# Two graph layers in one kernel: constants and tests at other places, other turns of the tiles for gathered rows, lists spread over three pairs

## The chip, the cores and the metric

The kernel runs on one core of one Trainium2 chip. The metric is the device time of the whole program in microseconds (us), as the median of several runs.

## What is computed

```
def layer0(x, adj):                       # x: 2708 x 1024, adj: 2708 x 2708 of 0 and 1
    q, k, v = x @ Wq.T + bq, x @ Wk.T + bk, x @ Wv.T + bv
    z = (q @ k.T) / sqrt(1024) * adj
    z = where(z == 0, -10000, z)
    return relu(softmax(z, axis=1) @ v)
x = layernorm(x + layer0(x, adj))
x = layernorm(x + (adj @ (x @ w1) + b1))
```

The adjacency is sparse and its degrees fall steeply with the row number: a few rows have many neighbours, most have a few, some have one or none.

## The kernel before

**The work.** Scores are needed only between a row and its neighbours. With M made once from Wq and Wk, a row's scores are the products of its row of y = xM (a broadcast row is added to it) with the rows of x of its neighbours. So the kernel first lists the neighbours of every row, and then gathers rows by indirect DMAs, which POOL (GpSimd) issues. The 22 blocks of 128 rows stand in two families, the first 8 and the other 14; inside a family rows are sorted by degree, and `SLOTS` says how many neighbours a block has room for. Rows of more neighbours go to a block of its own, the hub.

**The order of time.** (1) to 127 us: weights are loaded and M is made on PE, while DVE lists columns of the adjacency matrix. (2) 127 to 247 us: y of the first family, in four pairs (`y_pair(b)` for b = 0, 2, 4, 6). A pair is `pair_products` (L324), seven half products of a Strassen kind with sums that POOL makes beforehand (`y_sums_of`); PE's matmuls are at L300, and the sums that DVE adds to them at L322. DVE lists the last columns in the gaps: `list_columns` on DVE (L237), `count_columns` on ACT (L253). `sort_begin(f)` sorts a family by degree, `sort_end(f)` needs a small matmul on PE (L671) and gives the records, and `records_out` (L700) writes one record for each block by an indirect DMA, and then loads the table `tabs` (L710). A gather needs its block's table. (3) 247 to 460 us, the y stage: y of the other 14 blocks, block by block (L380; the last one at L431), copied from PSUM by ACT (L320) and stored by SP (L371). Beside it runs the attention of the first family's blocks and of the hub: ACT copies a broadcast row into a tile `yg` (L475), a gather adds the row of y to it (L464), the neighbours' rows of x are gathered into tiles `g` (L480), DVE makes a score from each (`score`, L1004), ACT the exponentials (L1040, L1131), and DVE the weighted sum `r` from the same tiles (L1061, L1138). (4) 461 to 747 us: the sums are turned by PE and multiplied by Wv, again in pairs; x is added (L1202), and ACT and DVE make the layernorm, whose rows POOL scatters to `x1_d` (L910). (5) 747 to 770 us: the last scatter, the first gathers from `x1_d`. (6) to 1070 us, layer 1: neighbours' rows of x1 are gathered and summed by DVE (L1429, L1432), turned by PE (L923), multiplied by w1, normed and scattered.

**What sets the order.** Attention of the blocks is cut into jobs that a planner runs between PE's blocks as their credit allows. Each engine runs its instructions in the order that results. `follow(put, what)` makes an instruction wait for an earlier one; `products` is the list of the last matmuls of PE's products, so that `products[-1]` is the newest and `products[-2]` the one before. `between[n]` holds what is to be issued behind product number n.

**Tiles.** A pool with `bufs=n` gives n tiles in turn, and a new use of one waits until its last reader is done. Gathered rows of x have `G1` = 9 tiles `g`; while there are blocks of y left, `g_tile` takes the two tiles `xr` of the pool `wp` as well, for 2 of 11. Gathered y has two tiles `yg`. Sums `r` have a ring of `RB` = 5.

**Row constants and tests.** The last part of the scores, a constant for each row, is made late: `row_constants` gathers x once more for 23 groups of rows (L464) and multiplies by a broadcast row `u_bc` on DVE (L1260), nine groups in the third-last pair of stage (4), nine in the second-last and five in the last; `single_scores` scores the two blocks with one neighbour. `test_scores` (L1271 on) then tests whether the short lists were enough and whether a score is exactly zero, for the result's flag; its work is a matmul on PE (L1287) and some 34 small steps on DVE (L1288 to L1309).

The lines that decide where these stand:

```
xg = gather_at(x, at, n, g_tile(), behind=products[-1])          # row_constants
if i == len(steps) - 3:
    u_bc = wp.tile([P, D], F32, name="u_bc", tag="yg")
    bcast_rows(u_bc, u_col)
if i >= len(steps) - 3:
    row_constants((9, 9, 5)[i - len(steps) + 3])
```

Of the kernel before, what the change touches and what calls it, by code (L numbers as in the profile page):

```python
# [9 lines left out]
F32 = mybir.dt.float32  # L10
BF16 = mybir.dt.bfloat16
I32 = mybir.dt.int32
# [9 lines left out]
P = 128  # L22
# [18 lines left out]
G1 = 9  # L41
# [40 lines left out]
def sparse_part(ctx, tc, x, xT, adj, wqT, wkT, wvT, bq, bk, bv, w1, b1, out):  # L82
# [28 lines left out]
    with es:  # L111
# [83 lines left out]
        recs = [lists.tile([P, nb, REC], I32, name=f"rec{f}") for f, nb in enumerate((FAMILY, NB - FAMILY))]  # L195
# [306 lines left out]
        def deal_hub():  # L502
# [51 lines left out]
            nc.gpsimd.dma_start(out=keys_d.rearrange("(p k) e -> p (k e)", k=KW), in_=keys)  # L554
# [14 lines left out]
            yield  # L569
            mm = p_mm.tile([P, HALF], F32, name="mm")  # L570
# [96 lines left out]
        def sort_end(f, behind=None):  # L667
            b0, nb = families[f]
            bs, NKB = slice(b0, b0 + nb), NK * nb
            before = spare_bank() if f else p_mm.tile([P, HALF], F32, name="mm")  # L670
            put = nc.tensor.matmul(before[:, :NKB], lower, hot_f[f], start=True, stop=True)  # L671
            if behind is not None:
                follow(put, behind, same=True)
            total = spare_bank()
            nc.tensor.matmul(total[:, :NKB], ones, hot_f[f], start=True, stop=True)
            one_row = lists.tile([P, NKB], F32, name=f"one_row{f}")
            nc.vector.memset(one_row, 1.0)
            upto = lists.tile([P, NKB], F32, name=f"upto{f}")
# [6 lines left out]
            pos_i = lists.tile([P, nb], I32, name=f"pos_i{f}")  # L685
            nc.vector.tensor_copy(pos_i, pos)

            rec = recs[f]
# [117 lines left out]
        y_sums = []  # L806
        t3 = yb.tile([P, DC // 2, HALF], F32, name="y_t3")
        y_sums.append(yb.tile([P, 4, DC // 2, P], F32, name="y_s0"))
        t4 = yb.tile([P, DC // 2, HALF], F32, name="y_t4")
        y_sums.append(yb.tile([P, 4, DC // 2, P], F32, name="y_s1"))  # L810
        nc.gpsimd.memset(yb.tile([P, 800], F32, name="cleared"), 0.0)
# [32 lines left out]
        sorted_late = []  # L844
# [39 lines left out]
        left_y, taken = NB - FAMILY, [0]  # L884
# [182 lines left out]
        def r_tile(b):  # L1067

            if b in FIRST:
                return wp.tile([P, D], F32, name="r", tag="t")  # L1070
            ring.append(b)
            return wp.tile([P, D], F32, name="r", bufs=RB)
# [32 lines left out]
        def attend_shares(b, got):  # L1105
# [7 lines left out]
            yg = gather_onto(b, y_bc, y_ds[0][:, :], rec[:, OFF:OFF + 1], P, wp.tile([P, D], F32, name="yg"))  # L1113
# [140 lines left out]

        def row_constants(count):
            for k in [c_left.pop(0) for _ in range(count)]:
                n = P if k in (0, NB) else rows[k]
                at = rec_h[:, ROW:ROW + 1] if k == NB else tab0[:, ROW:ROW + 1] if k == 0 else tabs[:n, k, ROW:ROW + 1]
                xg = gather_at(x, at, n, g_tile(), behind=products[-1])
                nc.vector.scalar_tensor_tensor(junkv[:n], xg[:n], 1.0, u_bc[:n], op0=ALU.mult, op1=ALU.mult,  # L1260
                                               accum_out=c_rows[:n, k:k + 1])
# [9 lines left out]
        def test_scores():  # L1271
# [5 lines left out]
            if rows[-1] < P:  # L1277
# [3 lines left out]
            nc.vector.tensor_tensor(over, degs, cap, op=ALU.is_gt)  # L1281
            s0, b0 = slot0[single[0]], single[0]
            nc.vector.scalar_tensor_tensor(nms[:, b0:b0 + len(single)], scores[:, s0:s0 + len(single)], -1.0,
                                           valid[:, b0:b0 + len(single), 0], op0=ALU.mult, op1=ALU.mult)
# [44 lines left out]
        for i, (kind, b) in enumerate(steps):  # L1329
# [29 lines left out]
            if kind == "y":  # L1359
                if FAMILY + 1 <= b < FAMILY + 7:  # L1360
                    next(deal)
                if b == FAMILY + 11:
# [18 lines left out]
            else:  # L1381
# [35 lines left out]
        def sum_rows(b, k=0, behind=None):  # L1417
            if b == "hub":
                n, tab, ok, r = P, tab_h, valid_h, part
            else:  # L1420
                n, tab, ok = (P, tab0, valid0) if b == 0 else (rows[b], tabs[:, b, :SLOTS[b]], valid[:, b, :SLOTS[b]])
                r = (cp if k else wp).tile([P, D], F32, name="r", bufs=3 if k else RB)
# [408 lines left out]
```

## Time and profile before

| | us |
|---|---|
| median of 5 runs | 1075.43 |
| lowest and highest | 1072.45, 1077.47 |
| the profiled execution | 1072.17 |
| its span | 1070.3 |
| PE busy | 962.7 (90%) |
| DVE busy | 836.2 (78%) |
| POOL busy | 557.0 (52%) |
| ACT busy | 410.8 (38%) |

The mean clock granted to PE is 0.958 of full speed. PE, DVE, ACT, POOL and SP are the five engines; POOL's busy time is the issuing of indirect DMAs. The page cuts the span into 40 slices and gives the busy share of each in tenths. A row of waits reads "engine line waited for what: us in total, times, longest". A row of a timeline reads "start, duration, engine, line, operation, tiles", and in brackets the idle time before it with what ended it. All line numbers are those of the kernel before.

### The profile page before, as it was taken

To read this page: it belongs to the slowest core of one execution; us is meant where nothing else is said; L and a number is where in the kernel's file an instruction comes from. 1 tells how busy PE (TensorE), PEld (TensorE's weight loads), DVE (VectorE), ACT (ScalarE), POOL (GpSimd) and SP (SyncE) were. 2 spreads that over 40 slices of the span, in tenths; PEclk is the share of its full clock that TensorE was granted. 3 is DMA by queue.
4 is the path that set the end of the run, shared out by engine and by line. 5 is a ranking of instruction groups with operands and counts; after the bars stand their busy time and mean duration, and the time that the engine had idled before them with its cause. 6 is when DMAs were issued, how large, how long until landed. Compare 5 with 4: busy or idle time off the path is not lost.

```text
span 1070.3 us, 10455 instructions
## 1 busy us (share of the span) xinstructions
PE 962.7 (90%) x2697; PEld 452.7 (42%) x2697; DVE 836.2 (78%) x2045; ACT 410.8 (38%) x917; POOL 557.0 (52%) x456
## 2 busy tenths in 40 slices
PE   8999869999998889899998999998299899989894
PEld 6444324444443334345544444443144344434441
DVE  8999999932857889957998899587869886868532
ACT  4453456432533324516343544422312343353521
POOL 0441452155676566105675753346588777768510
PEclk9999999999998989899999999999599999999998
DMA  9568775347987787217658874369898689987731
GB/s 353 183 205 249 221 240 165 121 148 219 278 232 247 232 252 227 103 43 234 174 157 226 226 236 159 113 237 354 289 276 238 205 294 279 327 240 218 212 110 42
DMA packets 103181, 229.21 MB, mean 214 GB/s; under 512 B 19774, under 2 KB 47174, under 8 KB 103112
## 3 DMA queue, kind: packets, MB, share of 16 engines
q0 software_dynamic: 51408, 159.09, 48.8%
q1 hardware_dynamic: 51704, 69.36, 20.1%
q8 instruction: 23, 0.38, 0.1%
q14 instruction: 46, 0.38, 0.1%
HBM read 218.08 MB, written 33.64 MB: 235 GB/s over the span
## 4 chain that ended last, share of the span: by engine, by line
PE 26%; DVE 23%; issue 20%; DMA 16%; POOL 12%; ACT 1%; POOLq 0%; SPq 0%; DVEq 0%; ACTq 0%
PE po L300 21%; POOL g L480 6%; DVE at_a L237 5%; DMA g<-in_x_dram,tabs 4%; DMA g<-x_d,tabs 3%; DVE junkv L1004 2%; PE po L380 2%; POOL xr L464 2%; DVE r L1061 2%; DMA out_dram<-t,tabs 1%; DMA a<-in_adj_dram 1%; POOL yg L464 1%; PE po L431 1%; DVE r L1432 1%; PE tr L923 1%
## 5 line engine op out<-in xcount | busy, mean ns | idle before, releaser
L380 PE MATMUL po<-m,xt 128*128 128x512 f32 x416 | 185.6, 606 | 15.1 <-ACT yo L320 15.1
L1004 DVE SCALAR_TENSOR_TENSOR junkv<-yg,g 128x1024 uint8<-128x1024 f32 x96 | 117.2, 1220 | 48.8 <-DMA g<-in_x_dram,tabs 21.4
L300 PE MATMUL po<-t,s_all 128*128 128x512 f32 x320 | 146.2, 600 | 7.6 <-DVE xr L322 6.3
L380 PEld LDWEIGHTS po<-m,xt 128*128 128x128 f32 x416 | 80.0, 195 | 118.0 <-issue 96.7
L480 POOL DMA_INDIRECT g<-in_x_dram,tabs x77 | 96.0, 1246 | 50.1 <-issue 15.2
L1432 DVE SCALAR_TENSOR_TENSOR r<-g,valid,r 128x1024 f32<-128x1024 f32 x77 | 98.2, 1280 | 21.1 <-DMA g<-x_d,tabs 18.5
L300 PEld LDWEIGHTS po<-t,s_all 128*128 128x128 f32 x320 | 60.5, 192 | 87.9 <-issue 70.2
L480 POOL DMA_INDIRECT g<-x_d,tabs x66 | 76.0, 1152 | 22.4 <-issue 14.9
L237 DVE FIND_INDEX8 at_a<-ones,a 128x8 uint16<-128x83 f32 (+3 forms) x132 | 82.6, 628 | 0.0
L966 ACT ACTIVATE junks<-t,lnm 128x1024 uint8<-128x1024 f32 (+1 forms) x40 | 45.9, 1148 | 93.8 <-DVE lnm L964 93.7
L300 PE MATMUL po<-w,rT 128*128 128x512 f32 x160 | 75.2, 611 | 3.1 <-DVE t L1469 3.1
L1061 DVE SCALAR_TENSOR_TENSOR r<-g,pr,r 128x1024 f32<-128x1024 f32 x58 | 73.7, 1279 | 4.4 <-ACT r L1059 4.3
L300 PE MATMUL po<-wv,s_all 128*128 128x512 f32 x160 | 73.9, 606 | 3.5 <-DVE t L322 3.4
L979 ACT ACTIVATE t<-t,nmr,rstd 128x1024 f32<-128x1024 f32 (+1 forms) x40 | 49.1, 1238 | 68.2 <-DVE nmr L978 68.2
L300 PE MATMUL po<-t,rT 128*128 128x512 f32 x160 | 73.3, 600 | 1.1 <-DVE t L1469 0.5
L253 ACT ACTIVATE junk<-a 128x2756 uint8<-128x2756 uint32 (+1 forms) x22 | 55.0, 2501 | 49.2 <-issue 17.0
L300 PE MATMUL po<-w,s_all 128*128 128x512 f32 x160 | 72.3, 592 | 0.0
L300 PE MATMUL po<-wv,rT 128*128 128x512 f32 x160 | 72.1, 600 | 0.0
L923 PE MATMUL tr<-ident,r 128*128 128x128 f32 x304 | 41.6, 286 | 31.6 <-DVE r L1429 23.5
L924 ACT COPY rT<-tr 128x512 f32<-128x512 f32 x76 | 41.4, 587 | 71.6 <-PE tr L923 70.3
L453 ACT ACTIVATE junka<-xt 128x128 f32<-128x128 f32 x168 | 51.7, 307 | 42.8 <-PE po L300 33.2
L464 POOL DMA_INDIRECT xr<-in_x_dram,tabs x22 | 27.5, 1252 | 63.3 <-DVE t L1202 31.2
(415 smaller groups left out, 1731.4 us busy)
## 6 DMA issues: line engine op xcount, KB each, us to landing
xt<-in_xT_dram SPq DMA_DIRECT2D x21, 512.0 KB, 5.3
y_d<-yo SPq DMA_DIRECT2D x21, 512.0 KB, 4.6
a<-in_adj_dram SPq DMA_DIRECT2D x21, 413.5 KB
a<-in_adj_dram SPq DMA_DIRECT2D x21, 338.5 KB, 3.6
a<-in_adj_dram SPq DMA_DIRECT2D x21, 263.5 KB, 4.6
wq_i<-in_wqT_dram SPq DMA_DIRECT2D x8, 512.0 KB, 4.8
wk_i<-in_wkT_dram SPq DMA_DIRECT2D x8, 512.0 KB, 10.5
wv<-in_wvT_dram SPq DMA_DIRECT2D x16, 256.0 KB, 5.7
```

Source lines behind the costliest of these rows:

```text
L237: nc.vector.max_index(at[:n, i], ones[:n, :8], a[:n, cuts[i] + 8 * i:cuts[i + 1] + 8 * i + 8])
L253: put = nc.scalar.activation(junk[:n], loaded[b][:n, :AW].bitcast(U32), AF.Sign, accum_out=cnt[:n, b:b + 1])
L300: put = nc.tensor.matmul(acc, a[:, k], w[:, k], start=start and k == 0, stop=stop and k == DC // 2 - 1, skip_group_check=True)
L380: put = nc.tensor.matmul(po, xts[b][:, c, :], m_q[c // 4][h][:, c % 4], start=(c == 0), stop=(c == DC - 1))
L453: put = nc.scalar.activation(junka[:, :xt.shape[2]], xt[:, c, :], AF.Copy, accum_out=xs[:, c, b:b + 1])
L464: put = nc.gpsimd.indirect_dma_start(out=dst[:n], out_offset=None, in_=src, in_offset=bass.IndirectOffsetOnAxis(ap=at, axis=0), compute_op=op)
L480: nc.gpsimd.indirect_dma_start(out=dst[:n], out_offset=None, in_=src, in_offset=bass.IndirectOffsetOnAxis(ap=at, axis=0), bounds_check=N - ...
L923: nc.tensor.transpose(tr[:, k, :], r[:, c * P:(c + 1) * P], ident)
L979: applied.append(nc.scalar.activation(t[:n], t[:n], AF.Identity, bias=nmr[:n], scale=rstd[:n]))
L1004: nc.vector.scalar_tensor_tensor(junkv[:n], yg[:n], scale, xg[:n], op0=ALU.mult, op1=ALU.mult, accum_out=s)
L1061: nc.vector.scalar_tensor_tensor(r[:n], xg[j][:n], pr[:n, j:j + 1], r[:n], op0=ALU.mult, op1=ALU.add)
L1432: put = nc.vector.scalar_tensor_tensor(r[:n], xg[:n], ok[:n, j:j + 1], r[:n], op0=ALU.mult, op1=ALU.add)
```

## The change

Four things are changed. *Constants and tests*: the gathers of `row_constants` wait for the product before the newest one; `u_bc` is broadcast one step sooner, into `part` (the hub's sum) in place of a tile `yg`; the first steps of `test_scores` on DVE and its matmul wait for the newest product, which puts them behind products of layer 1. *Tiles of gathered y*: `y_tile` gives four in turn, two `yg` and the two `xr`, while blocks of y are left. *Tiles of gathered x*: `g_tile` gives nine tiles, each with its own tag, in a fixed turn, and no longer borrows `xr`; the ring of `r` gets a pool of its own. *Lists*: the last eight columns are listed three, three and two over the pairs b = 0, 2 and 4 instead of four and four over b = 0 and 2; `sort_begin(1)` comes behind b = 4 and `sort_end(1)` behind the last pair; the 14 records of the second family are written two at a time behind the y blocks 2 to 8 of stage (3) instead of in a row before it; `keys_d` is written from SP's queue instead of POOL's. Record tiles move into another pool, and a `memset` goes.

```diff
@@ hub's keys
-            nc.gpsimd.dma_start(out=keys_d.rearrange("(p k) e -> p (k e)", k=KW), in_=keys)
...
+            follow(nc.sync.dma_start(out=keys_d.rearrange("(p k) e -> p (k e)", k=KW), in_=keys), products[-2])
@@ y pairs
-            if done < NB:
-                list_columns()
-                list_columns()
-                done += 4
-                for k in (1, 3, 5, 7):
-                    between[first + k] = [count_columns]
-                for k in (2, 4):
-                    between[first + k] = [lambda put: list_columns()]
+            for k in range(min(3, NB - done)):
+                if k:
+                    between[first + 2 * k] = [lambda put: list_columns()]
+                else:
+                    list_columns()
+                done += 1
+                between[first + 2 * k + 1] = [count_columns]
             if b == 4:
-                between[first + 6] = [lambda put: sorted_late.append(sort_end(1, put))]
+                between[first + 4] = [lambda put: next(deal)]
...
             if b == 2:
                 load_last()
+                bcast_rows(y_bc, y_col)
+            if b == 4:
                 sort_begin(1)
-                bcast_rows(y_bc, y_col)
-            if b in (0, 2, 6):
+            if b in (0, 6):
                 next(deal)
...
-            if b == 4:
-                records_out(*sorted_late[0], 0, NB - FAMILY)
+        later_records = sort_end(1, products[-1])
@@ tiles
+        rp = es.enter_context(tc.tile_pool(name="sums", bufs=RB, reuse_waits="tile"))
 
         def g_tile():
 
-            taken[0] += 1
-            if left_y and taken[0] % (G1 + 2) in (4, 9):
-                return wp.tile([P, D], F32, name="xr", bufs=2)
-            return gp.tile([P, D], F32, name="g", tag="g")
+            filled[1] += 1
+            return gp.tile([P, D], F32, name="g", tag=f"g{filled[1] % G1}", bufs=1)
 
+        def y_tile():
+
+            filled[0] += 1
+            if left_y and filled[0] % 4 in (3, 0):
+                return wp.tile([P, D], F32, name="xr", bufs=2)
+            return wp.tile([P, D], F32, name="yg")
+
         def gather_y(b):
             return gather_onto(b, y_bc, y_ds[b >= FAMILY][:, :], tabs[:rows[b], b, OFF:OFF + 1], rows[b],
-                               wp.tile([P, D], F32, name="yg"))
+                               y_tile())
@@ constants and tests
+        u_bc = part
...
-                xg = gather_at(x, at, n, g_tile(), behind=products[-1])
+                xg = gather_at(x, at, n, g_tile(), behind=products[-2])
...
-            nc.vector.tensor_tensor(over, degs, cap, op=ALU.is_gt)
+            follow(nc.vector.tensor_tensor(over, degs, cap, op=ALU.is_gt), products[-1])
...
-            nc.tensor.matmul(mm[:, :1], ones, bqk, start=True, stop=True)
+            follow(nc.tensor.matmul(mm[:, :1], ones, bqk, start=True, stop=True), products[-1], same=True)
@@ steps
                 if FAMILY + 1 <= b < FAMILY + 7:
                     next(deal)
+                if 2 <= b - FAMILY < 9:
+                    records_out(*later_records, 2 * (b - FAMILY - 2), 2 * (b - FAMILY - 2) + 2, products[-2])
...
-                if i == len(steps) - 3:
-                    u_bc = wp.tile([P, D], F32, name="u_bc", tag="yg")
+                if i == len(steps) - 4:
                     bcast_rows(u_bc, u_col)
                 if i >= len(steps) - 3:
                     row_constants((9, 9, 5)[i - len(steps) + 3])
```

More of the change, by code (lines that the diff above doesn't have):

```diff
@@ L194, in sparse_part @@
         keys = lists.tile([P, NB, KEYS], F32, name="keys")
-        recs = [lists.tile([P, nb, REC], I32, name=f"rec{f}") for f, nb in enumerate((FAMILY, NB - FAMILY))]
         nc.vector.memset(cnt, float(8 * RANGES))
@@ L684, in sort_end @@
             nc.vector.tensor_reduce(pos, by_class(upto, nb).rearrange("p k b -> p b k"), AX.X, ALU.add)
-            pos_i = lists.tile([P, nb], I32, name=f"pos_i{f}")
+            pos_i = (xa if f else lists).tile([P, nb], I32, name=f"pos_i{f}", bufs=1)
             nc.vector.tensor_copy(pos_i, pos)
-            rec = recs[f]
+            rec = (xa if f else lists).tile([P, nb, REC], I32, name=f"rec{f}", bufs=1)
             nc.vector.memset(rec[:, :, ROW:], 0)
@@ L806, in sparse_part @@
         y_sums = []
+        y_sums.append(yb.tile([P, 4, DC // 2, P], F32, name="y_s0"))
         t3 = yb.tile([P, DC // 2, HALF], F32, name="y_t3")
-        y_sums.append(yb.tile([P, 4, DC // 2, P], F32, name="y_s0"))
         t4 = yb.tile([P, DC // 2, HALF], F32, name="y_t4")
         y_sums.append(yb.tile([P, 4, DC // 2, P], F32, name="y_s1"))
-        nc.gpsimd.memset(yb.tile([P, 800], F32, name="cleared"), 0.0)
         nc.vector.tensor_sub(t3, t2, m_q[0][0])
@@ L843, in sparse_part @@
         wv_q = [None, quarters_of("wv", (1,))[0]]
-        sorted_late = []
         while counted[0] < done:
@@ L883, in sparse_part @@
         gp = es.enter_context(tc.tile_pool(name="g0", bufs=G1, reuse_waits="tile"))
-        left_y, taken = NB - FAMILY, [0]
+        rp = es.enter_context(tc.tile_pool(name="sums", bufs=RB, reuse_waits="tile"))
+        left_y, filled = NB - FAMILY, [0, 0]
         bias_bc = hp.tile([P, D], F32, name="bias_bc", tag="bias")
@@ L1071, in r_tile @@
             ring.append(b)
-            return wp.tile([P, D], F32, name="r", bufs=RB)
+            return rp.tile([P, D], F32, name="r")
         def mean_rows(b):
@@ L1112, in attend_shares @@
                 r = r_tile(b)
-            yg = gather_onto(b, y_bc, y_ds[0][:, :], rec[:, OFF:OFF + 1], P, wp.tile([P, D], F32, name="yg"))
+            yg = gather_onto(b, y_bc, y_ds[0][:, :], rec[:, OFF:OFF + 1], P, y_tile())
             for i, (j0, j1) in enumerate(pieces(J)):
@@ L1280, in test_scores @@
             over = stat.tile([P, NB], F32, name="over", bufs=1)
-            nc.vector.tensor_tensor(over, degs, cap, op=ALU.is_gt)
+            follow(nc.vector.tensor_tensor(over, degs, cap, op=ALU.is_gt), products[-1])
             s0, b0 = slot0[single[0]], single[0]
-            nc.vector.scalar_tensor_tensor(nms[:, b0:b0 + len(single)], scores[:, s0:s0 + len(single)], -1.0,
-                                           valid[:, b0:b0 + len(single), 0], op0=ALU.mult, op1=ALU.mult)
+            put = nc.vector.scalar_tensor_tensor(nms[:, b0:b0 + len(single)], scores[:, s0:s0 + len(single)], -1.0,
+                                                 valid[:, b0:b0 + len(single), 0], op0=ALU.mult, op1=ALU.mult)
+            follow(put, products[-1])
             mm = p_mm.tile([P, HALF], F32, name="mm")
-            nc.tensor.matmul(mm[:, :1], ones, bqk, start=True, stop=True)
+            follow(nc.tensor.matmul(mm[:, :1], ones, bqk, start=True, stop=True), products[-1], same=True)
             nc.vector.tensor_scalar(c_rows, c_rows, mm[:, :1], None, op0=ALU.add)
@@ L1421, in sum_rows @@
                 n, tab, ok = (P, tab0, valid0) if b == 0 else (rows[b], tabs[:, b, :SLOTS[b]], valid[:, b, :SLOTS[b]])
-                r = (cp if k else wp).tile([P, D], F32, name="r", bufs=3 if k else RB)
+                r = (cp if k else rp).tile([P, D], F32, name="r", bufs=3 if k else RB)
             for j in range(tab.shape[1] if b else J0):
```

## The prediction

> **What bounds the kernel now.** I read the page's slices first, then the waits of each stage, then timelines at the three places that the change touches.
>
> ```profile
> span 1070.3 us, 10455 instructions
> PE   8999869999998889899998999998299899989894
> DVE  8999999932857889957998899587869886868532
> POOL 0441452155676566105675753346588777768510
> ```
>
> Each digit is 26.8 us. PE is the bound nearly everywhere, so a part of the change is worth only what it takes out of PE's gaps. There are three groups of gaps: the y pairs (127 to 247 us), the y stage of single blocks (247 to 460) and the hole after slice 28, which is the passage from layer 0 to layer 1.
>
> The waits of the y pairs, the y stage (247 to 440) and the end of layer 0 (700 to 772), as total, times, longest:
>
> ```profile
> PE po L300 <- DVE yo L322: 11.2, 2, 10.1
> ...
> ACT yg L475 <- DVE junkv L1004: 48.3, 6, 13.0
> DVE junkv L1004 <- DMA g<-in_x_dram,tabs: 17.2, 10, 4.2
> DVE junkv L1004 <- DMA yg<-y_d,tabs: 17.0, 2, 15.5
> PE po L380 <- ACT yo L320: 15.1, 5, 5.1
> POOL yg L464 <- ACT yg L475: 8.8, 4, 4.7
> PE po L431 <- ACT yo L320: 6.0, 1, 6.0
> ...
> PE tr L923 <- DVE r L1429: 23.5, 1, 23.5
> PE po L300 <- DVE t L322: 3.8, 2, 2.8
> ```
>
> In the y stage PE loses 15.1 + 6.0 = 21.1 us to copies of y that stand on ACT behind an exponential; that waits for DVE's scores; those wait for gathered rows. So the chain there is gathers (POOL) to scores (DVE) to ACT to PE. DVE's first score starts at 268.38, after 15.5 us of waiting for gathered y.
>
> The passage, as timelines of DVE and POOL (start, duration, engine, line, idle before):
>
> ```profile
> 750.85 1.23 DVE L1004 SCALAR_TENSOR_TENSOR junkv<-g 128x1024 uint8<-128x1024 f32 x1 [1.63 <-DMA g<-in_x_dram,tabs]
> 752.79 0.67 DVE L322 TENSOR_TENSOR t<-po,t 128x512 f32<-128x512 f32 x1
> 757.23 1.23 DVE L1260 SCALAR_TENSOR_TENSOR junkv<-g,u_bc 128x1024 uint8<-128x1024 f32 x1 [2.05 <-DMA g<-in_x_dram,tabs]
> 764.55 0.24 DVE L1288 TENSOR_SCALAR c_rows<-c_rows,mm 128x23 f32<-128x23 f32 x1
> ...
> 761.56 1.19 POOL L910 DMA_INDIRECT x_d<-t,tabs  x1 [4.73 <-ACT t L997]
> 765.38 1.03 POOL L480 DMA_INDIRECT g<-x_d,tabs  x1 [2.62 <-DMA x_d<-t,tabs]
> ```
>
> PE's last product of layer 0 ends at 746.87. Its add (752.79) stands on DVE behind a single's score that waits for its gather, and the norm that follows stands behind row constants that wait for theirs.
>
> **Part 1, constants a pair sooner: the passage.** In the order of the changed kernel all 23 constants and both single scores stand ahead of the last add on DVE, and the last five gathers wait for a product that ended 12.3 us before the last one (734.61 to 746.87). What is left behind the last product: up to 0.6 us of adds in hand; add to mean-and-variance 2.40 (752.79 to 755.19); ACT's two small steps 0.79 (755.47 to 755.98, with its start); four small DVE steps 0.85; ACT's half of the scaling 0.81; 0.52 until the scatter starts. That is 6.0, so the scatter starts at 752.9 instead of 761.56, 8.7 sooner; landing, gather and first sum follow as before. Bounds: 9.5 (nothing in hand) and 4 (if x1's landing, 2.62 after the issue, or the five gathers' traffic is late). **-8.7.**
>
> Ahead of it, DVE waits 0.2 to 1.34 us for nearly every constant's gather, and PE's 3.8 us at L322 are these. Gathers a product sooner take most of it: **-2.5** (0 to -3.8). The broadcast copy now goes into the hub's sum, a tile that is free by then; nothing waits for it.
>
> **Part 2, tests behind a unit of layer 1.** 4.6 us of DVE (764.55 to 769.18) leave the passage. They were hidden there: DVE still sat 0.41 us before x1's rows came at 769.60. With 8.7 us gone they would have been the next thing late, so part 1 needs part 2. In layer 1 DVE is busy 12.9 and 18.0 of 20 us in 940 to 960 and 960 to 980, and PE waits there for DVE once, 3.07 us. All of it on the path costs 4.6, none 0 (it can't gain, as the passage is already counted); I take **+1**, nearer to none, since DVE has 9.1 us of gaps there.
>
> **Part 3, lists over three pairs.** 8 columns at some 5.7 us of DVE each are the same work. PE's 10.1 us stall at 161.91 waits for an add of the first pair; the changed order still has three columns' work ahead of that add, so I keep the stall (bounds -10 and +3). Pair b=4 now has list work and the hub's keys in front of its adds; pair b=2 and the hot-column matmul (1.8) gain. **+1** for the stage.
>
> The 14 record writes leave POOL's queue at 222.44 to 239.87 and stand in pairs in the y stage. What was queued behind them were the first gathers of x, six of them (3 MB) issued from 242.79 on. They moved beside the last y stores: 13 us at 314 GB/s, and the first gather of y could start only at 260.05. Four of the six can now go some 20 us earlier, for their table was in place long before: 2 MB less at 314 GB/s is **-6.7** for the first score (0 to -8.3).
>
> Price of the writes where they now stand: 14 x (0.96 + 0.30) = 17.6 us of POOL. POOL's idle time, less 0.30 for each of its instructions, is 6.4 in 260 to 300, 6.6 in 300 to 345, 15.1 in 345 to 390 and 9.3 in 390 to 433. Eight writes (10.1 us) fall into the first two, where 13 us are free but partly wait on releases; six into the third, which covers them. What overflows delays gathers that DVE waits for: **+4** (0 to +17.6). Their wait for a product is no cost: in the times of before, each product named ends 20 us or more ahead of the DVE step that the gather in front of the write waits for.
>
> The keys' store goes from POOL, which sat 15.59 us ahead of it at 217.42, to SP's queue behind the last but one product; on SP only loads and y stores are near: 0.
>
> Here the row shows gathers of one size taking 0.99 us on POOL at 245.47, where DVE has no scores, and 1.6 to 2.0 beside its scores (1.75 at 407.92). The Trainium skill, SBUF — State Buffer, section "SBUF: two separate sides", says that descriptors of a DMA issued from GpSimd can't be written while DVE holds the shared port pair, which speaks against moving writes next to scores. By it a write could cost as much as the slow gathers. The sum by that: 14 x (2.0 + 0.3) = 32 instead of 17.6; the stage's small reads, 0.94 mostly, speak against it. The sum keeps 0.96, from the writes' own rows.
>
> **Part 4, tiles.** Gathered x had 9 tiles and 2 borrowed; now 9 in fixed turn. A tile serves two heavy DVE steps (a score and a sum, 1.25 us apart), so two fewer tiles take four steps from the lead between a tile's release and its next use: 9 or 10 in the order of before where the queue was free, 4 to 6 in that of the changed kernel. How much lead is needed:
>
> ```profile
> 407.92 1.75 POOL L480 DMA_INDIRECT g<-in_x_dram,tab x1 [4.37 <-DVE part L1138]
> ...
> 413.08 1.23 DVE L1004 SCALAR_TENSOR_TENSOR junkv<-yg,g 128x1024 uint8<-128x1024 f32 x1 [1.71 <-DMA g<-in_x_dram,tab]
> ```
>
> This gather, with a lead of four, took 5.16 us to its use and cost 1.71. Leads of five or fewer rise by my count from 10 to 28. At 1.71 each the 18 more cost 31, with none late 0, and a shorter lead gains nothing; most are fives (6.25 us against 5.2 to 7.7 measured), so 0.35 each: **+6**.
>
> The page DMA: Bandwidth & Descriptors of the Trainium skill, section "Anatomy of one DMA — SWDGE (gpsimd) path", fits such a DMA as 2.0 us plus its bytes at 436 GB/s, 3.2 us for 512 KB. By that a lead of four would be enough and this term nothing; the row of 5.16 decides.
>
> Gathered y has four tiles instead of two: the next block's copy on ACT no longer waits for the last score on the old tile, and POOL no longer stands 8.8 us before those gathers. But ACT's y copies follow nearly the same DVE steps in both orders, so I give **-3** (0 to -8.8).
>
> The y stage together: -6.7 + 4 + 6 - 3 = +0.3. What is late next is again DVE waiting for x.
>
> **The sum.** 1 + 0.3 - 2.5 - 8.7 + 1 = -8.9 on the profiled execution's 1072.17 (span 1070.3) gives 1063.3. That execution lies 3.3 below the median 1075.43: **1066.5**.
>
> **The rivals.** A, slower: in the y stage the nine tiles and the record writes make gathers the bound. One cycle of a tile then sets DVE's pace: each of the 18 shorter leads costs 1.0 (+12 on my term) and the eight writes in the dense part cost in full (+6): 1066.5 + 18 = 1084. It turns the whole slower once the stage ends more than 12.4 us later than before, 9.2 of the other parts and 3.2 of uncertainty. For it: 18 us of DVE's 25 us of waiting for gathered x fell between 294 and 352, just where POOL issued without a break. Against it: PE has 21.1 us of its own waiting there, and POOL's last 90 us have room.
>
> B, faster: the y copies come on time, since y's tiles end ACT's blocking. Of PE's 21.1 us, 14 go: 1052. For it the 48.3 us of ACT at L475; against it the unchanged DVE steps.
>
> C, the change doesn't do what it says: the constants' waits only move a pair forward into PE's adds (the 3.8 grows by as much as the passage loses): some 1074, no change.
>
> **How the numbers follow.** Forecast 0.47 (1060 to 1073), B 0.14, C 0.12, A 0.27. A measurement tells 0.3% (3.2 us) from no change. Faster: 0.44 + 0.14 = 0.58; same: 0.03 + 0.12 = 0.15; slower: 0.27. The range reaches to most of A and B: 1050 to 1084.
>
> **What would show it.** PE's wait at the passage near 15 instead of 23.5, with no L1264 after the last add; first score near 262; the 3.8 gone. DVE's waiting for gathered x in the y stage is 25.0 now (17.2 and 7.8 in smaller rows); some 30 means the leads, 40 or more means A. I am wrong if y's last block starts after 445 instead of 433, or if the passage stays above 20.

## The result, and the profile after

The changed kernel takes 1079.5 us (median of 52 runs, 1072.74 to 1084.75) against 1075.78 us (94 runs of the kernel before beside it). The ratio is 1.003, 95% interval [1.0021, 1.004]: slower by some 3 us, where 9 us less was forecast; the measured time lies 13 us above the 1066.5 of the forecast. Its profiled execution took 1079.87 us, with a span of 1078.1 at a granted clock of 0.959.

The page's span and PE's slices:

```profile
span 1078.1 us, 10444 instructions
PE   7999869999999678779999979998499999989894
```

The hole in the slices is now a 4 instead of a 2, so it is shorter, as forecast; new 6, 7 and 8 stand in the middle. PE's and DVE's waits of the y stage (246 to 440 or 470), of the pairs of stage 4 (462 to 745) and of their end with the passage (745 to 790), as total, times, longest:

```profile
PE po L379 <- ACT yo L319: 22.4, 6, 10.6
PE po L430 <- ACT yo L319: 7.9, 1, 7.9
...
DVE junkv L1006 <- DMA g<-in_x_dram,tabs: 26.5, 13, 4.9
DVE junkv L1006 <- DMA g<-in_x_dram,tab_h: 7.7, 5, 2.3
DVE junkv L1006 <- DMA g<-in_x_dram,tab: 6.6, 6, 2.5
DVE junkv L1006 <- DMA yg<-y_d,tabs: 5.2, 1, 5.2
...
PE po L299 <- DVE t L321: 14.3, 7, 6.0
PE po L299 <- DVE nms L1033: 2.4, 1, 2.4
PE tr L925 <- ACT rT L926: 1.0, 1, 1.0
...
PE tr L925 <- DVE r L1435: 14.4, 1, 14.4
PE po L299 <- DVE t L321: 4.1, 1, 4.1
```

PE's waits in the pairs of the kernel before (462 to 745):

```profile
PE po L300 <- DVE t L322: 4.9, 4, 2.8
PE tr L923 <- DVE r L1061: 3.5, 1, 3.5
PE tr L923 <- ACT rT L924: 1.8, 1, 1.8
```

Read against the rows of before: the passage lost 9.1 us of PE's waiting (23.5 to 14.4). PE's waits in the y stage rose from 21.1 to 30.3 and DVE's waits for gathered x there from 25 to 40, though the first score starts at 255.10 instead of 268.38. And the pairs, with 10.2 us of waits over the whole stage before, have 21.8 now (14.3, 2.4, 1.0 and the 4.1, which still belongs to the last pair).

The table puts the two kernels and the ones tried below side by side. A row is one profiled execution, and one execution differs from the next by some 5 us: layer 1, after the passage, takes from 297 to 306 us in these profiles. So times are judged by the ratios, and only the stages are read here. *y from* is the start of the first matmul of the y stage; *y stage* runs from there to the start of its last block; *x* is DVE's waiting for gathered x in it; *pairs* runs from the last matmul at L380 to the end of layer 0's last product, *PE* is PE's waiting in it; *hole* is PE's wait in the passage. "e4, nine x tiles" means e4 with that one difference.

| kernel | ratio | y from | first score | y stage | x | pairs | PE | hole |
|---|---|---|---|---|---|---|---|---|
| before | 1 | 246.8 | 268.4 | 186.4 | 25.0 | 287.8 | 10.2 | 23.5 |
| after | 1.003 | 242.9 | 255.1 | 194.8 | 40.1 | 302.5 | 21.8 | 14.4 |
| e1 constants, tests | 0.9918 | 246.8 | 268.2 | 190.0 | 27.0 | 293.7 | 13.9 | 13.8 |
| e2 tiles | 1.0083 | 246.8 | 263.9 | 192.7 | 35.6 | 294.8 | 16.0 | 24.5 |
| e3 lists | 0.9978 | 242.8 | 256.7 | 188.6 | 33.8 | 289.2 | 12.4 | 26.1 |
| e4 all but tiles | 0.9893 | 242.8 | 257.4 | 189.5 | 34.0 | 293.8 | 14.2 | 14.4 |
| e5 e4, nine x tiles | 0.9978 | 242.9 | 257.3 | 194.6 | 36.5 | 291.9 | 12.3 | 14.3 |
| e6 constants | 0.9932 | 245.5 | 267.0 | 187.6 | 25.9 | 293.2 | 12.6 | 14.2 |
| e8 all but lists | 1.0024 | 246.6 | 263.4 | 191.4 | 35.0 | 301.0 | 20.9 | 13.9 |
| e15 after, x by pool | 0.9967 | 243.5 | 256.3 | 196.8 | 39.6 | 294.0 | 14.2 | 14.3 |
| e16 e4, records twice | 1.0064 | 243.3 | 257.6 | 203.4 | 44.5 | 290.0 | 13.2 | 14.0 |
| e17 e4, records later | 0.9861 | 243.8 | 258.1 | 185.8 | 28.4 | 292.3 | 13.3 | 14.5 |

### The profile page after: what moved, and what is told of

Same layout as the page of the kernel before. It is cut to its first block, busy times and chain, and to the rows that moved or that the text cites. A ratio compares the mean times of both kernels' runs of the same rounds, so it can differ in the third digit from the quotient of the medians.

```text
span 1078.1 us, 10444 instructions
## 1 busy us (share of the span) xinstructions
PE 962.1 (89%) x2697; PEld 451.3 (42%) x2697; DVE 833.9 (77%) x2045; ACT 409.3 (38%) x917; POOL 557.7 (52%) x454
## 4 chain that ended last, share of the span: by engine, by line
PE 28%; DVE 24%; issue 18%; DMA 17%; POOL 11%; ACT 1%; POOLq 0%; SPq 0%; DVEq 0%; ACTq 0%
PE po L299 18%; PE po L379 9%; DVE at_a L236 5%; POOL g L479 4%; DMA g<-in_x_dram,tabs 4%; DVE junkv L1006 3%; DMA xr<-x_d,tabs 3%; DVE r L1063 2%; POOL g L463 2%; DMA g<-x_d,tabs 2%; POOL xr L463 2%; DVE t L321 1%; DMA yg<-y_d,tabs 1%; DMA g<-in_x_dram,tab_h 1%; DMA a<-in_adj_dram 1%
## 5 line engine op out<-in xcount | busy, mean ns | idle before, releaser
L299 PE MATMUL po<-t,s_all 128*128 128x512 f32 x320 | 149.1, 610 | 13.0 <-DVE t L321 7.4
L479 POOL DMA_INDIRECT g<-in_x_dram,tabs x84 | 111.6, 1329 | 47.5 <-issue 15.6
L1006 DVE SCALAR_TENSOR_TENSOR junkv<-yg,g 128x1024 uint8<-128x1024 f32 x69 | 84.2, 1221 | 40.9 <-DMA g<-in_x_dram,tabs 22.6
L299 PE MATMUL po<-wv,s_all 128*128 128x512 f32 x160 | 76.4, 623 | 12.6 <-DVE t L321 10.1
L1063 DVE SCALAR_TENSOR_TENSOR r<-g,pr,r 128x1024 f32<-128x1024 f32 x64 | 81.6, 1280 | 2.0 <-ACT r L1061 1.6
L1006 DVE SCALAR_TENSOR_TENSOR junkv<-xr,g 128x1024 uint8<-128x1024 f32 x37 | 45.3, 1224 | 26.5 <-DMA g<-in_x_dram,tabs 11.6
```

The source lines that it names most:

```text
L299: put = nc.tensor.matmul(acc, a[:, k], w[:, k], start=start and k == 0, stop=stop and k == DC // 2 - 1, skip_group_check=True)
L479: nc.gpsimd.indirect_dma_start(out=dst[:n], out_offset=None, in_=src, in_offset=bass.IndirectOffsetOnAxis(ap=at, axis=0), bounds_check=N - ...
L1006: nc.vector.scalar_tensor_tensor(junkv[:n], yg[:n], scale, xg[:n], op0=ALU.mult, op1=ALU.mult, accum_out=s)
L1063: nc.vector.scalar_tensor_tensor(r[:n], xg[j][:n], pr[:n, j:j + 1], r[:n], op0=ALU.mult, op1=ALU.add)
```

## The experiments

**The parts by themselves.** The diff falls into three parts: the constants and tests, the tiles, the lists and records. First each of them alone on the kernel before, and all without the tiles. In all of them the one `memset` stays, and the order of two tiles beside it is that of before. (They stay so in e8 further down too, which is as slow as the changed kernel.)

e1_const_tests, only this of the change:

```diff
+        u_bc = part
...
-                xg = gather_at(x, at, n, g_tile(), behind=products[-1])
+                xg = gather_at(x, at, n, g_tile(), behind=products[-2])
...
+            follow(nc.vector.tensor_tensor(over, degs, cap, op=ALU.is_gt), products[-1])
```

> The kernel before with the constants' gathers a product sooner and the tests behind a unit of layer 1, nothing else of the change. The passage from layer 0 to layer 1 took PE 23.5 us in the kernel before and 14.4 us in the changed one. Theory 1 (these two parts gain and the rest of the change loses): the passage is near 14.5 us, the pair stage loses no more than its 10 us of waits, and the time is 8 to 11 us under the kernel before. Theory 2 (the passage is shorter only because its work was pushed into the pair stage, whose waits on DVE grew from 10 to 26 us): the pair stage is longer by 5 us or more here too, and the time is within 5 us of the kernel before.

1069.92 us against 1077.21, ratio 0.9918 [0.9888, 0.9948]: 8.8 us gained. The hole is 13.8. The pairs are 6 us longer, so some of the passage's work may cost there, as theory 2 has it, but not all of it.

e2_tiles, only `y_tile`, the fixed turn of `g_tile` and the sums' pool:

```diff
+            filled[1] += 1
+            return gp.tile([P, D], F32, name="g", tag=f"g{filled[1] % G1}", bufs=1)
...
+            if left_y and filled[0] % 4 in (3, 0):
+                return wp.tile([P, D], F32, name="xr", bufs=2)
```

> The kernel before with four tiles for gathered y, nine tiles in fixed turn for gathered x and a pool of their own for the sums, nothing else of the change. Theory 1 (the shorter leads of nine tiles and the order that comes with them cost): the y stage, 186.5 us to the last block's start before and 194.8 us after, is 8 us longer, the pair stage up to 14 us longer, and the time is 8 to 20 us over the kernel before. Theory 2 (the tiles cost nothing, and the record writes in the y stage do): within 4 us of the kernel before.

1086.79 us, ratio 1.0083 [1.0055, 1.011]: 9 us lost, by 6 us in the y stage and 7 in the pairs. Theory 1.

e3_lists, only the lists, the sort behind them, the records and the keys' store:

```diff
+            for k in range(min(3, NB - done)):
...
+                    records_out(*later_records, 2 * (b - FAMILY - 2), 2 * (b - FAMILY - 2) + 2, products[-2])
```

> The kernel before with the columns listed over three pairs, the second family's sort behind them and its records written two at a time in the y stage, and the keys stored from SP's queue; one memset stays. Theory 1 (the tiles cost, the lists do not): the first score at some 262 us instead of 268, and the time within 4 us of the kernel before or up to 7 us under it. Theory 2 (14 writes of 1.26 us each on a POOL that was full between 287 and 347 us hold the gathers up): the y stage 8 us longer and the time 6 to 14 us over the kernel before.

1075.91 us, ratio 0.9978 [0.9948, 1.0008]: no change that can be told. The y stage begins 4 us sooner and the first score 11.7 us sooner, but the stage is 2.2 us longer: the scores' head start does not reach its end. DVE waits 8.8 us more for gathered x there.

e4_no_tiles, the changed kernel with the old tiles:

```diff
-            filled[1] += 1
-            return gp.tile([P, D], F32, name="g", tag=f"g{filled[1] % G1}", bufs=1)
+            taken[0] += 1
+            if left_y and taken[0] % (G1 + 2) in (4, 9):
+                return wp.tile([P, D], F32, name="xr", bufs=2)
+            return gp.tile([P, D], F32, name="g", tag="g")
```

> The changed kernel with the tiles as they were (two for gathered y, nine and two borrowed for gathered x), one memset kept. Theory 1 (the tiles lose what the constants gain): 8 to 16 us under the kernel before, near 1064. Theory 2 (the lists and records lose it): as slow as the changed kernel, within 4 us of 1079.

1067.42 us, ratio 0.9893 [0.9854, 0.9932]. Without the tiles' part the change gains 11 us. So that part loses 9 us by itself (e2) and 15 on top of the others (e4 against the changed kernel), and it is the reason for the result.

**What in the tiles' part costs.** Three things are in it. e5_nine_x takes one of them alone on e4:

```diff
-            if left_y and taken[0] % (G1 + 2) in (4, 9):
-                return wp.tile([P, D], F32, name="xr", bufs=2)
             return gp.tile([P, D], F32, name="g", tag="g")
```

> The kernel without the tiles' part (constants, tests and lists changed, 0.989 of the kernel before), but with nine tiles for gathered x and none borrowed; gathered y keeps its two tiles, so that two tiles lie idle in the y stage. Theory 1 (the shorter lead of gathered x is what costs): most of the loss of the tiles' part comes back, 7 to 12 us over that kernel, ratio 0.996 to 1.001. Theory 2 (the four tiles for gathered y cost, since y is gathered sooner and its scores are put ahead of PE's adds in the pair stage): within 3 us of that kernel, ratio 0.987 to 0.992.

1072.6 us, ratio 0.9978 [0.9951, 1.0005] against 0.9893 for e4. The y stage is 5.1 us longer, the pairs are not. Theory 1 for the y stage; the rest of the 9 us between the two ratios is in no stage that these two profiles can tell.

e8_no_lists, the changed kernel with the old lists and records:

> The changed kernel with the lists and records as they were. Theory 1 (tiles +9, lists within 3 us): 1075 to 1080, ratio 0.997 to 1.004 of the kernel before, so the lists matter little beside the tiles too. Theory 2 (record writes on POOL only hurt when leads are short): faster than the changed kernel by 4 us or more, ratio under 0.998.

1076.38 us, ratio 1.0024 [1.0002, 1.0045], as slow as the changed kernel. Lists and records make no difference beside the tiles. The pairs are at 301 here too.

e9_y_four_once, the changed kernel with

```diff
-            if left_y and filled[0] % 4 in (3, 0):
+            if filled[0] in (3, 4):
```

> The changed kernel, but the two further tiles for gathered y are taken once only, for the third and the fourth gather; the hub's, block 0's and all later rows of y use the two old tiles. Theory 1 (what the four tiles cost is the early gathering at the end of the y stage, which puts scores of the next blocks on DVE ahead of PE's adds in the pair stage): the pair stage falls from 302 us to some 292, and the time to that of nine tiles with two for y, ratio 0.996 to 0.999 of the kernel before. Theory 2 (the pair stage is longer for another reason, the constants or the late end of the y stage): within 3 us of the changed kernel, ratio 1.001 to 1.005.

1080.6 us, ratio 1.0031 [1.0003, 1.0059], pairs 301.2: theory 2. It is not the late use of y's tiles.

e11_seven_x, e4 with seven tiles for x in the y stage:

```diff
+            turns = G1 if taken[0] <= G1 or not left_y else G1 - 2
+            return gp.tile([P, D], F32, name="g", tag=f"g{taken[0] % turns}", bufs=1)
```

> The kernel without the tiles' part, with seven tiles for gathered x in the y stage (nine for the first turn and later on); two for y. Theory 1 (time follows the lead of gathered x): going from eleven to nine cost 5 us in the y stage and 9 in all; each two tiles take four heavy steps (5 us) from every lead, and a lead of about one step leaves 5 us of each gather open, so the y stage is 20 to 45 us longer than with nine and DVE's waiting for gathered x there over 60 us. Theory 2 (the order that came with nine tiles cost, not the lead): within 8 us of nine tiles.

1103.33 us, ratio 1.0229 [1.0184, 1.0273], 36 us over e4. Fewer tiles do cost more, but not as theory 1 has it: the y stage is 198.9, only 4.3 us over nine tiles, with 45.3 us of DVE's waiting for x instead of over 60. The pairs are at 319. PE waits 21.1 us for DVE's adds there. That DVE is late at the end of the y stage, and takes attention work along into the pairs, would explain it, but this kernel also has the fixed turn, which the next runs show to matter there; the two are not separated.

Then the changed kernel with one of the three things put back.

e13_y_two, two tiles for y:

> The changed kernel with two tiles for gathered y. Theory 1 (four tiles for y cost in the pair stage): the pair stage falls from 302 us to some 292 and DVE's waiting for gathered y there from 12 to 6, ratio 0.996 to 0.999 of the kernel before. Theory 2 (the sums' pool or the fixed turn cost): pair stage at 300 or more, ratio 1.001 to 1.005.

1079.74 us, ratio 1.0014 [0.999, 1.0039]; y stage 194.2, pairs 298.5, DVE's waiting for gathered y in the pairs 12.2. Nothing that can be told from the changed kernel, so theory 1 of that run falls.

e14_sums_back, `rp.tile(...)` back to `wp.tile(..., bufs=RB)`:

> The changed kernel with the ring of sums back in the pool with the other tiles, four tiles for y and nine in fixed turn for x kept. Theory 1 (y's tiles): no change, ratio 1.001 to 1.005. Theory 2 (the sums' own pool changes what PE turns when, and so costs in the pair stage): pair stage near 292, ratio 0.996 to 0.999.

1079.88 us, ratio 1.0038 [1.0007, 1.0068]; pairs 301.0. No change.

e15_x_by_pool, one line:

```diff
-            return gp.tile([P, D], F32, name="g", tag=f"g{filled[1] % G1}", bufs=1)
+            return gp.tile([P, D], F32, name="g", tag="g")
```

> The changed kernel with nine tiles for gathered x given out by the pool as they come free instead of in fixed turn. Theory 1 (y's tiles) and theory 2 (the sums' pool): no change, ratio 1.001 to 1.005. Theory 3 (the fixed turn costs, since a gather waits for its own tile even where another is free): pair stage near 292, ratio 0.996 to 0.999.

1074.88 us, ratio 0.9967 [0.9943, 0.999]: 6 to 7 us under the changed kernel. Theory 3. The pairs fall from 302.5 to 294.0, the y stage keeps its length. Waits of DVE and PE in the pairs of this kernel (462 to 745):

```profile
DVE junkv L1006 <- DMA yg<-y_d,tabs: 4.5, 2, 2.8
...
PE po L299 <- DVE t L321: 4.0, 7, 1.4
```

The changed kernel has 12.6 us in three for the first row and 14.3 in seven for the second. The longest of the first row, from DVE's timeline of the pairs in the changed kernel, and POOL's instructions ahead of it:

```profile
480.23 1.23 DVE L1006 SCALAR_TENSOR_TENSOR junkv<-yg,g 128x1024 uint8<-128x1024 f32 x1 [7.58 <-DMA yg<-y_d,tabs]
...
472.51 0.91 POOL L463 DMA_INDIRECT xr<-in_x_dram,tabs  x1 [4.50 <-DMA y_d<-yo]
473.72 1.60 POOL L463 DMA_INDIRECT yg<-y_d,tabs  x1 [0.30 <-issue]
```

In the order that comes with the fixed turn, the first scores on the second family's rows of y stand on DVE ahead of the adds that PE waits for, and the gather of those rows stands on POOL behind one of x that waits for the last y store. The add at 482.65 stands behind two of these scores, the next, at 485.01, behind a third, and PE goes on at 485.75, after a stall of 6.0 us. In e15 POOL waits for that store as well (8.4 us, until 470.39), and the gather of y starts at 471.59; but DVE's order there is another, with the first add ahead of the first of these scores:

```profile
474.90 0.69 DVE L321 TENSOR_TENSOR t<-po,t 128x512 f32<-128x512 f32 x1 [2.74 <-PE po L299]
...
499.47 1.22 DVE L1006 SCALAR_TENSOR_TENSOR junkv<-yg,g 128x1024 uint8<-128x1024 f32 x1
```

PE has no such stall there. A second stall of the changed kernel, 5.1 us until 630.09, is gone in e15 too. Why the fixed turn leads to this order is not shown.

**The record writes.** e16_records_twice, e4 with each record of the y stage written a second time, into a table that nothing reads (the call in the y stage has `twice=True`):

```diff
-            for b in range(k0, k1):
+            for b, to in [(b_, to_) for b_ in range(k0, k1) for to_ in [tab_ds[f]] + [tab_twin] * twice]:
```

> The kernel without the tiles' part, each of the 14 records of the y stage written twice, the second time into a table that nothing reads (so 14 more instructions of 0.96 us and 0.30 between). If a write costs what the prediction gave it (4 us for the 14), 2 to 6 us over that kernel; if POOL's time is the bound of the y stage's middle, 8 to 18 us over it, and DVE's waiting for gathered x in the y stage rises from 34 us to over 40.

1084.26 us, ratio 1.0064 [1.0037, 1.009] against 0.9893: 14 more writes cost 18 us, the y stage alone 13.9, of which PE's waits are 11.3. That is 1.3 us a write, and a write's row on POOL has 0.96 + 0.30. The largest single waits of DVE, here and in e4, come at the same score (waits of the y stage, e16 first, the last number is the longest):

```profile
DVE junkv L1003 <- DMA g<-in_x_dram,tabs: 33.1, 8, 13.6
```

```profile
DVE junkv L1001 <- DMA g<-in_x_dram,tabs: 21.3, 5, 10.9
```

and e4's timeline of POOL ahead of that wait, which ends at 307.37, shows why: nothing but small instructions for 13 us, four of them record writes, with gathers of y and x queued behind them.

```profile
285.40 1.65 POOL L463 DMA_INDIRECT rec_h<-tab_d,row_i  x1 [0.30 <-PE po L379]
287.35 1.99 POOL L463 DMA_INDIRECT found<-keys_d,at_i  x1 [0.30 <-issue]
289.65 0.94 POOL L463 DMA_INDIRECT found<-keys_d,at_i  x1 [0.30 <-issue]
...
292.15 2.02 POOL L699 DMA_INDIRECT tab_d<-rec,pos_i  x1 [0.30 <-DMA found<-keys_d,at_i]
294.48 0.97 POOL L699 DMA_INDIRECT tab_d<-rec,pos_i  x1 [0.30 <-issue]
...
297.01 0.96 POOL L699 DMA_INDIRECT tab_d<-rec,pos_i  x1 [0.30 <-issue]
298.28 1.61 POOL L463 DMA_INDIRECT yg<-y_d,tabs  x1 [0.31 <-issue]
```

e17_records_later, e4 with the writes two y blocks later:

```diff
-                if 2 <= b - FAMILY < 9:
-                    records_out(*later_records, 2 * (b - FAMILY - 2), 2 * (b - FAMILY - 2) + 2, products[-2])
+                if 4 <= b - FAMILY < 11:
+                    records_out(*later_records, 2 * (b - FAMILY - 4), 2 * (b - FAMILY - 4) + 2, products[-2])
```

> The kernel without the tiles' part (0.9893 of the kernel before), its records written behind the y blocks 4 to 10 of the stage instead of 2 to 8. If the place counts (POOL full from some 285 to 330 us, with gaps later), DVE's waiting for gathered x in the y stage falls from 34 us to 28 or less and 3 to 8 us are gained, ratio 0.982 to 0.987. If each write costs its time on POOL wherever it stands, the ratio stays at 0.987 to 0.992.

1062.15 us against 1074.3, ratio 0.9861 [0.9827, 0.9895]: the fastest version here, 1.4% under the kernel before. The interval touches e4's, so the time alone does not settle the place. The profile does: the y stage is 185.8 instead of 189.5, the wait for x 28.4 instead of 34.0 (33.6 to 35.2 in e3, e4, e10 and e12, all four with the writes at the earlier place and the old tiles), and the longest wait of 10.9 is gone:

```profile
DVE junkv L1001 <- DMA g<-in_x_dram,tabs: 12.1, 8, 2.7
```

**The tests.** e6_const_only, e1 with the tests left in the passage:

> The kernel before with the constants' gathers a product sooner, and the tests left in the passage. If the tests (4.6 us of DVE steps) are the next thing late there, as the prediction has it, the passage is 4 us longer than with both parts (13.8 us in that kernel, so 17 to 19 here), and the time 3 to 5 us over it: ratio 0.995 to 0.997 against 0.992. If the tests are hidden there all the same, the ratio is 0.991 to 0.993.

1067.89 us, ratio 0.9932 [0.9907, 0.9957], not to be told from e1's 0.9918; the hole is 14.2. DVE's timeline of the passage in that kernel, the last step of the tests but two and the first sum of layer 1:

```profile
757.74 0.16 DVE L1308 TENSOR_TENSOR some<-some,bad 128x1 f32<-128x1 f32 x1
...
764.23 0.97 DVE L1430 TENSOR_SCALAR r<-g,valid 128x1024 f32<-128x1024 f32 x1 [5.95 <-DMA g<-x_d,tabs]
```

The tests still fit under the landing of x1's rows, with 5.95 us to spare.

e12_const_lists, the same with the lists changed:

> Constants and lists changed, the tests left in the passage and the tiles as they were. If the tests' new place is worth nothing: as without the tiles' part, ratio 0.987 to 0.992. If the tests hold the shorter passage up: 0.992 to 0.996.

1071.16 us, ratio 0.992 [0.9889, 0.9951]. It lies between the two expectations, and the interval overlaps e4's. Together with e6: the tests' new place is worth nothing that these runs can tell.

**The first pair's stall.** The change leaves the longest wait of the y pairs as it was (10.1 before, 10.5 after). e7_lists_2_3_3 lists two, three and three columns:

```diff
-            for k in range(min(3, NB - done)):
+            for k in range(min(3 if b else 2, NB - done)):
```

> The kernel without the tiles' part, with the eight columns listed two, three and three over the pairs instead of three, three and two. The stall of 10.5 us in the first y pair, which waits for an add on DVE, is untouched by the change. If it is the lists that stand ahead of that add (5.7 us of DVE each), one column fewer takes 5 to 6 us from it and the time is 3 to 6 us under that kernel, ratio 0.984 to 0.987. If what stands there is other work, or the third pair now stalls as much, the ratio stays at 0.988 to 0.991.

4784.53 us. It says nothing on the question: with three columns in the third pair, a later entry of `between` took the place of one listing, a column stayed unlisted, and the kernel went its long way for graphs that the lists can't hold. e10_lists_2_3_3 moves that entry from `first + 4` to `first + 6`:

> The kernel without the tiles' part, with the eight columns listed two, three and three over the pairs; all eight are listed this time (in the run e7_lists_2_3_3 a later entry took the place of one listing, so that kernel missed a column, and it went its long way for graphs that the lists can't hold). If columns' work is what the first pair's add waits for (stall 10.5 us), 5 to 6 us of it go: ratio 0.984 to 0.987 of the kernel before. If the third pair stalls as much instead, 0.988 to 0.991.

1072.97 us, ratio 0.9928 [0.9894, 0.9963], no better than e4. The stall is still there, 11.4 us. What the first pair's add waits for is not set by how many columns are given to that pair. DVE's timelines say what stands there: columns all the same. Ahead of that add 17 of the 22 columns and most of an 18th are listed, in the kernel before, in e4 and in e10 alike, though e10 gives only 16 to the first pair and what lies before it: columns of the next pair moved up. Why the order puts them there was not found.

## Why the prediction was wrong, point by point

**By parts.** Against the prediction's terms, in time: constants and tests forecast -10.2 (-2.5 - 8.7 + 1), measured -8.8 by themselves (e1); lists and records forecast -1.7 (1 - 6.7 + 4), measured -2.4, which can't be told from nothing (e3); tiles forecast +3 (6 - 3), measured +9 by themselves (e2) and +15 on top of the others (e4). So the step that failed is the tiles' term: it priced the lead of gathered x in the y stage, and had nothing for what the fixed turn does to the order of the instructions in the pairs. The terms in turn:

**The passage (-8.7) was right.** The steps came out as they were added up. DVE's timeline of the changed kernel, then POOL's:

```profile
766.10 0.69 DVE L321 TENSOR_TENSOR t<-po,t 128x512 f32<-128x512 f32 x1 [0.45 <-PE po L299]
...
769.93 0.55 DVE L1000 TENSOR_SCALAR t<-t,rstd,nmr 128x512 f32<-128x512 f32 x1
...
771.22 0.95 POOL L912 DMA_INDIRECT x_d<-t,tabs  x1 [2.88 <-ACT t L999]
775.30 1.03 POOL L479 DMA_INDIRECT g<-x_d,tabs  x1 [3.13 <-DMA x_d<-t,tabs]
```

The last product ends at 766.06, and the scatter starts 5.2 us later, where 6.0 was added up. The hole is 9.1 us shorter. One reading under this term was wrong, without effect on the sum: 734.61 is the start of a product in the middle of the last pair, and the product that the last five gathers wait for had ended at 718, 29 us before the last one and not 12.3.

**The constants ahead of it (-2.5) had the wrong sign.** The pairs are 5.4 us longer with the constants alone (e6: 287.8 to 293.2). PE's waits grew by 2.4 to 3.7 of that (e6, e1); the largest is now in the last pair, 3.5 us in e6, for an add that stands on DVE among the five constants that had been in the passage. The step that failed is that gathers a product sooner would take these waits away. The other 3 us are not waits: PE is busy 280.4 us in this stage of e6 and 277.1 before, with the same number of matmuls and a granted clock of 0.98 instead of 0.99. e16, which has the constants' change too, has 276.5 at 0.99, so these 3 us can't be put down to it, and their cause stays open. Rival C named the mechanism and overrated it. In time the constants by themselves gain 7.3 us (e6).

**The start of the scores (-6.7) was too small, and bought little.** Counted from the y stage's start, the first score comes 7.7 us sooner with the lists alone (21.6 to 13.9), and the y stage begins 4 us sooner besides. In e3 the stage is 2.2 us longer all the same, and even in e17 only 0.6 shorter than before. The step that failed is the one that carried a sooner start to the end of the stage unchanged.

**The record writes (+4) were mis-sized.** They were priced by POOL's idle time, as if the idle time of a stretch could be used anywhere in it. e16 prices 14 further writes at 14 us of the stage and 18 in all, the upper bound of 17.6 that the text had; the first 14 were not priced by themselves. In e3 9.9 us are lost between the first score and the stage's end (7.7 sooner, 2.2 later). e17 gets 3.7 of this stage back by moving the writes, so their place counts; what eats the rest is not shown. That start, writes and lists together came out near their forecast (-1.7; e3's stages have -4.0 to the y stage and +2.2 in it) is luck: each of the three was off, and the errors cancel.

**The tiles: the lead (+6) came out near, the turn was not in the sum.** Nine tiles cost 5.1 us in the y stage (e5), near the 6 forecast. That it is by the lead is not shown: two tiles less again add 4.3 to that stage (e11), where the same count of leads asked for 20 to 45. But the fixed turn costs 8.5 us of the pair stage and 6 to 7 in time (e15), by an order of the gathers and of DVE's scores that the prediction had not followed beyond the y stage. Four tiles for y, forecast at -3, are worth nothing that can be told (e13).

**Lists in the y pairs (+1):** the y stage starts 3.9 us sooner instead; PE's wait for the hot columns (1.8 us) and its stall at 214.11 (1.1 us) are gone, the long stall stayed as forecast, and the rest of the 3.9 was not traced. **Tests (+1):** nothing to be told, and the reason given was wrong: they would not have been next in the passage.

In sum, against forecast terms of 1, 0.3, -2.5, -8.7 and 1, the profile has -3.9 to the start of the y stage, +8.4 in it, +14.7 in the pairs, -9.1 in the passage and -2.2 in layer 1. That is 7.8 us between two single executions; the medians lie some 3 us apart. Most of the miss is in the pairs, for which the sum had -2.5: the constants' change goes with some 5 us there (e6), the fixed turn costs 8.5 (e15).

Rival A, the slower one, was near in its number, 1084, by luck. Its sign came (DVE waits 40.1 us for gathered x in the y stage), but that stage lost 8.4 us where A had some 18, and its last block started 4.5 us late (437.71 instead of 433.25) where A needed 12.4. What made the whole slower came in the pairs, and A does not have it. Neither of the two signs of being wrong appeared: y's last block started before 445, and the passage fell below 20. Neither looks at the pairs, where most of the loss was. That the turn is what costs in the pairs rests on one line (e15); y's tiles taken late (e9), y's tiles at all (e13) and the sums' pool (e14) had been tried and changed nothing that can be told.

## What to carry to other kernels

A change to the turn of buffers changed the order of later instructions on POOL and DVE here: follow the order of the changed kernel through the next stage too, and look there for waits that stand ahead of the bounding engine's adds. An instruction put on a queue cost about its full time here where that queue issues without a break, whatever the idle time of the stretch around it; look for the place with gaps (here two blocks later took 3.7 us off the stage). A sooner start of a stage is not a sooner end: look at what bounds its middle. And choose the signs of being wrong in every stage that the change can reach.

## What was not expected of the hardware

Small indirect DMAs are as dear on POOL as gathers many times their size: a read of one word for each of 128 rows takes 0.94 us (`found` in e4), a record write of 28 words for each takes 0.96, and a gather of 512 KB 0.99, each with 0.30 us to the next. Some take about twice that: in e4's rows above a read at 287.35 takes 1.99 us and a write at 292.15 takes 2.02, and DVE makes a score of 1.2 us beside each of them. But the read of 0.94 at 289.65 has a score beside it too, so a score beside it is not enough. 18 us of time for 14 more writes (e16) is 1.3 us each.
